# Attention in a transformer block: another order of projections, scores and context, and queries and keys stored token by token

## The chip, the core and the metric

The kernel runs on one core of a Trainium2 chip. The metric is the time of one execution on the device in microseconds (us); less is better. The engines of a core are named as in the profile: PE (TensorE, matrix products; PEld is its weight load), DVE (VectorE), ACT (ScalarE), POOL (GpSimd) and SP (SyncE, which here only issues DMAs). Each engine works through its own queue in order and waits on semaphores for the others.

## The reference

One block of a transformer on 2048 tokens of width 1024, in float32: layer norm, attention, residual, layer norm, gated feed-forward, residual. The attention is unusual: it runs within a token, over the token's 32 heads of width 32, not between tokens. So for every token there is a 32 x 32 matrix of scores, a softmax over it, and a 32 x 32 by 32 x 32 product with the values.

```python
x = L0_attn_hidden_states                       # (1, 2048, 1024)
x = x + attn(_layernorm(x, axis=-1), wq, bq, wk, bk, wv, bv, wl, bl)
x = x + ffn(_layernorm(x, axis=-1), w1, w2, w3)

def attn(hidden_states, ...):
    q = (hidden_states @ wq.T + bq).reshape(B, S, H, D)     # H = D = 32
    k = (hidden_states @ wk.T + bk).reshape(B, S, H, D)
    v = (hidden_states @ wv.T + bv).reshape(B, S, H, D)
    scores = jnp.einsum('bshd,bstd->bsht', q, k) / np.sqrt(D)
    probs = jax.nn.softmax(scores, axis=-1)
    return jnp.einsum('bsht,bstd->bshd', probs, v).reshape(B, S, E)

def ffn(x, w1, w2, w3):                                     # hidden width 2752
    dq1, dq2, dq3 = (nf4_quant_dequant(w) for w in (w1, w2, w3))
    h = silu(x @ dq1.T) * (x @ dq2.T)
    return h @ dq3.T
```

`nf4_quant_dequant` scales each block of 64 weights by its largest magnitude, rounds it to one of 16 values and scales it back.

## The kernel before

The tokens are worked on in 16 tiles of 128 (NT = 16, i is the tile). The program first runs a fast version of the block, in which the three projections use a float32 product with the activations split into a high and a low part (`xh`, `xl`); only if the weights are not what that needs does a second version run. The profile shows the fast one, and the change is in it.

The attention of a tile is made of these steps. The letters are functions in the code, and PE runs their products in exactly the order in which they are called, since PE's order is written by hand; on the other engines a scheduler places the instructions that each step issues, and may move them among each other.

- `prepare(i)`: layer norm of the tile on ACT and POOL, giving `xn`. The tile's input `xt` is loaded three tiles ahead, in `G(i-3,1)`.
- `split(i)`: eight PE transposes of `xn` (L618), which ACT and DVE copy as `xh` (L620) and `xl` (L621).
- `Q(i,n)`, `K(i,n)`, `V(i,n)`: half a projection each (n is the half of the columns), 16 products of 512 columns (L648) into one of four PSUM banks; then `take` on DVE moves the bank to SBUF, transposing blocks of 32 x 32 (L665 for queries and keys, L678 for values), and after the second half adds the bias (L667, L683). There is one buffer each for queries `qd`, keys `kd` and values `vd`.
- `S(i,part)`: scores of half of the tile's tokens, 64 products of 32 x 32 (L696). After the second half follows the softmax: DVE takes the maximum and subtracts it (L733, L735), ACT takes the exponential (L741), DVE transposes (L743), giving `prT`.
- `G(i,part)`: context of half of the tokens, 64 products of 32 x 32 by 32 x 33 (L700; the 33rd column of `vd` is all ones and gives the softmax's sum). After the second half DVE divides by the sum (L758, L760), transposes (L768) and adds the residual (L771); SP stores the result and loads the next input tile; POOL and ACT make the second layer norm (L578 to L585).
- `keep(i)`: eight PE transposes of the normed tile (L511), ACT copies, DVE differences (L527), and stores for the feed-forward.

Scores and context of all tiles share one PSUM tile `at` of four banks: it takes the scores of tile i, then its context, then the scores of tile i+1.

The loop over tiles calls, for i from 3 on:

```python
Q(i, 0); Q(i, 1); flush(1); keep(i - 2); K(i, 0)
G(i - 1, 0); K(i, 1); flush(1); G(i - 1, 1)
V(i, 0); S(i, 0); V(i, 1); flush(1); split(i + 1); S(i, 1); advance(2)
```

Between these steps the weights of the feed-forward are rounded in the background. `advance(n)` issues n x 10/17 turns of that work: a turn is mostly one of eight bands of a weight tile, one pass of ACT (L299) and one of DVE (L305), or a tile's scaling, sixteen small ACT instructions (L259). `flush` issues the four PE transposes of a finished weight tile's half (L219). Every projection, S and G calls `advance(1)`.

After the loop, the first products of the feed-forward (`plain_block`, eight groups of L391, taken one at a time by `next(plain)`) are mixed with the last tile's context and the last two `keep`s. There `held["behind"]` makes the background work wait for the last tile's norm. The feed-forward proper then runs to the end.

Of the kernel before, what the change touches and what calls it, by code (L numbers as in the profile page):

```python
# [16 lines left out]
ALU = mybir.AluOpType  # L17
# [3 lines left out]
P = 128  # L21
S = 2048
E = 1024
NH = 32
D = 32
# [5 lines left out]
NT = S // P  # L31
# [99 lines left out]
def forward(ctx, tc, const, fast, x, wqT, wkT, wvT, qb, kb, vb, w1, w2, w3, out):  # L131
# [113 lines left out]
    def flush(steps=3):  # L245
        for _ in range(steps):
            if pending and next(pending[0], flush) is flush:
                pending.pop(0)
# [108 lines left out]
    def advance(n):  # L357
        lent["turns"] += n * TURN
        while lent["turns"] >= 1:
            lent["turns"] -= 1  # L360
            with turn():
                next(bg, None)
# [80 lines left out]
    def load_op(name, tbp):  # L443
        tag = "T1" if name == "B12" else name
        t = wpool.tile([P, 4, TB], FP, tag=tag, name=f"x{name}")
        nc.sync.dma_start(t, xd[name, tbp])
        ops[tag] = (name, tbp, t)
# [83 lines left out]
    if fast:  # L531
# [78 lines left out]
        def split(i):  # L610

            hi = work.tile([P, KC, P], F32R, tag="xh", name="xh", bufs=2)
            lo = work.tile([P, KC, P], F32R, tag="xl", name="xl", bufs=2)
            src = xn.pop(i)
            for half in range(2):
                pt = bank("pt").rearrange("p (k t) -> p k t", t=P)
                for k in range(4):
                    nc.tensor.transpose(pt[:, k, :], src[:, ts(4 * half + k, P)], ident)  # L618
                ks = ts(half, 4)
                marked(nc.scalar.copy(hi[:, ks], pt))  # L620
                nc.vector.tensor_tensor(lo[:, ks], pt, hi[:, ks].bitcast(FP), ALU.subtract)  # L621
            xs[i] = hi, lo
# [17 lines left out]
                for n in range(2):  # L640
                    take(n, ps[i, n])

        def project(m, i, n, take):

            ps = bank("pj")
            for k in range(KC):
                for part in xs[i]:
                    nc.tensor.matmul(  # L648
                        ps,
                        part[:, k, :],  # L650
                        W[m][k // 2][:, k % 2, ts(n, TB)],
                        start=k == 0 and part is xs[i][0],
                        stop=k == KC - 1 and part is xs[i][1],
                        skip_group_check=True,
                    )
            take(n, ps)
            advance(1)

        def qk(m, i, bias):
            tag = f"{m}d" if i != 1 else "xT1" if m == "q" else "xT0"  # L660
            t = work.tile([P, 32, NH], FP, tag=tag, name=f"{m}d")

            def take(n, ps):
                hs = ts(n, NH // 2)
                nc.vector.transpose(t[:, hs], ps.rearrange("p (h d) -> p h d", d=D))  # L665
                if n:
                    nc.vector.tensor_tensor(  # L667
                        t, t, bias.unsqueeze(2).to_broadcast([P, 32, 32]), ALU.add
                    )

            return t, take
# [21 lines left out]

        def score(at, q, k, part):
            for s, b, n, r in tokens(part):
                nc.tensor.matmul(at[r, b, ts(n, 32)], q[r, :, s], k[r, :, s], start=True, stop=True)  # L696

        def weigh(at, p, part):
            for s, b, n, r in tokens(part):
# [3 lines left out]

        qd, kd, prT, ats = {}, {}, {}, {}

        def Q(i, n):
            if not n:
                qd[i] = qk("q", i, qb_sb)
            project("q", i, n, qd[i][1])

        def K(i, n):
            if not n:
                kd[i] = qk("k", i, kb_sb)
            project("k", i, n, kd[i][1])

        def V(i, n):
            project("v", i, n, take_v)
            if n:
                del xs[i]

        def S(i, part):

            if not part:
                ats[i] = ps_at.tile([P, 4, 512], FP, tag="at", name="sc")
            at = ats[i]
            score(at, qd[i][0], kd[i][0], part)
            advance(1)
            if not part:
                return
            del qd[i], kd[i], ats[i]  # L730
            sc = at[:, :, 0:256].rearrange("p g (s t) -> p g s t", t=NH)
            mx = small.tile([P, 4, 8], FP, tag="mx", name="mx")
            nc.vector.tensor_reduce(mx, sc, AX.X, ALU.max)  # L733
            pr = work.tile([P, 32, NH], FP, tag="pr", name="pr")
            nc.vector.tensor_tensor(  # L735
                pr.rearrange("p (g s) t -> p g s t", g=4),
                sc,
                mx.unsqueeze(3).to_broadcast([P, 4, 8, NH]),
                ALU.subtract,
            )  # L740
            nc.scalar.activation(pr, pr, AF.Exp, scale=1.0 / math.sqrt(D))  # L741
            prT[i] = work.tile([P, 32, NH], FP, tag="prT", name="prT")
            nc.vector.transpose(prT[i], pr)  # L743
# [37 lines left out]
        def keep(i):  # L781
            keep_T(i, x1n.pop(i))
# [36 lines left out]
        G(0, 1)  # L819
        prepare(3)  # L820
        V(1, 0)
        S(1, 0)
        V(1, 1)
        S(1, 1)
        K(2, 1)
        keep(0)
        split(3)
        for i in range(2, NT):
            last = i == NT - 1
            if i > 2:  # L830
                if not last:
                    prepare(i + 1)
                Q(i, 0)
                Q(i, 1)
                flush(1)
                keep(i - 2)
                K(i, 0)
            if last:
                for name in ("B11", "B21"):
                    load_op(name, 0)  # L840
            G(i - 1, 0)
            if i > 2:
                K(i, 1)
            flush(1)
            G(i - 1, 1)
            if last:
                until("2", 0)
                w0 = []
                for n, tag in enumerate(("xh", "xl")):
                    t = work.tile([P, 2, 4, P], FP, tag=tag, name="w0", bufs=2)  # L850
                    nc.sync.dma_start(t, wd["2", 0][:, 2 * n : 2 * n + 2])
                    w0 += [t[:, 0], t[:, 1]]
                for name in ("B12", "B22"):
                    load_op(name, 0)
            V(i, 0)
            S(i, 0)
            V(i, 1)
            flush(1)
            if not last and i > 2:
                split(i + 1)  # L860
            S(i, 1)
            advance(2)
        hook["scale"] = "both"
        left.close()
# [10 lines left out]
        hook["pool"] = (ps_tail, "pj", 2)  # L875

        plain = plain_block(w0, 0)
        next(plain)
        advance(1)
        next(plain)  # L880
        keep(NT - 2)
        advance(1)
        next(plain)
        G(NT - 1, 0)
        next(plain)
        G(NT - 1, 1)
        held["behind"] = hook["normed"]
        for _ in range(3):
            next(plain)
            advance(2)  # L890
        keep(NT - 1)
        hs = {0: next(plain)}
        advance(2)
        sweep.close()
        sweep_at.close()
        right.close()
# [806 lines left out]
```

## Time and profile before

| | |
|---|---|
| time, three runs | 2238.79, 2229.97, 2224.99 us (median 2229.97) |
| time of the profiled execution | 2238.77 us |
| its span, first to last instruction | 2236.9 us |
| PE busy | 2167.1 us (97%) |
| DVE busy | 1378.0 us (62%) |
| ACT busy | 1287.2 us (58%) |
| POOL busy | 302.2 us (14%) |
| mean granted clock of PE | 0.984 |

How to read it: busy is the time in which the engine had at least one instruction under way. The profile's line numbers are those of the kernel. In a group, `out<-in` names the tiles written and read; "x4096 | 67.6, 225 | 21.3 <-..." stands for 4096 records, 67.6 us busy in all, 225 ns for one, and 21.3 us in which the engine was idle just before them, with what ended that idleness. A product in float32 leaves two records, so half a tile's 64 small products are 128 records. PE's clock is granted in two steps here, full and half, and is listed as a share.

### The profile page before, as it was taken

The page shows a single profiled execution, that of the slowest core. Times are in us where ns is not written, and L with a number is a line of the kernel's source. Part 1 is how long each engine was busy: PE and PEld are TensorE (multiplying, and loading weights), DVE is VectorE, ACT ScalarE, POOL GpSimd, SP SyncE. Part 2 cuts the span into 40 slices and gives each one's busy share as a digit, 9 for nine tenths or more (in the row PEclk, how much of TensorE's full clock was granted, in tenths as well). Part 3 has the DMA queues.
Part 4 walks back from the last instruction along what each step waited for, and adds up shares of the span by engine and source line. Part 5 has one row for each costly group of instructions (what it writes and reads, how often), then busy time and mean ns, then how long its engine had stood idle before and what let it go on. Part 6 is the DMA issues. An engine that isn't in the chain of part 4 may idle for free.

```text
span 2236.9 us, 35174 instructions
## 1 busy us (share of the span) xinstructions
PE 2167.1 (97%) x14193; PEld 1173.4 (52%) x14193; DVE 1378.0 (62%) x1600; ACT 1287.2 (58%) x2529; POOL 302.2 (14%) x425
## 2 busy tenths in 40 slices
PE   7999999989989999999999999999999999999998
PEld 6777787778534444444444444444444444444432
DVE  6778777786377565576565665756666656653022
ACT  7566665662285756758657666676586575511200
POOL 2010010100001203104012021040130210401300
PEclk9899999999999999999999999999999999999999
DMA  8132323234558837579349596394883776974972
GB/s 292 40 101 93 117 65 115 95 98 144 216 193 294 172 141 180 163 280 252 137 141 210 206 283 149 124 214 162 308 207 133 181 190 224 269 236 136 255 290 96
DMA packets 154683, 402.72 MB, mean 180 GB/s; under 512 B 13648, under 2 KB 67920, under 8 KB 137360
## 3 DMA queue, kind: packets, MB, share of 16 engines
q1 hardware_dynamic: 113808, 326.92, 40.7%
q0 software_dynamic: 40704, 73.47, 19.7%
q8 instruction: 113, 1.85, 0.3%
q14 instruction: 58, 0.48, 0.1%
HBM read 227.07 MB, written 173.28 MB: 179 GB/s over the span
## 4 chain that ended last, share of the span: by engine, by line
PE 48%; issue 14%; DMA 5%; DVE 2%; ACT 2%; POOL 1%; DVEq 0%; POOLq 0%; ACTq 0%; SPq 0%
PE z L391 18%; PE q L391 8%; PE z L1511 8%; PE rr L391 4%; PE y L1511 4%; DMA wd<-wop 3%; DMA x1d<-acc 3%; PE r L1511 2%; PE po L1594 1%; PE ptw L219 1%; DVE r L305 1%; PE po L1605 1%; ACT wn L259 1%; POOL x1d L1526 1%; ACT acc L1524 0%
## 5 line engine op out<-in xcount | busy, mean ns | idle before, releaser
L299 ACT ACTIVATE sg<-wn 128x1024 int8<-128x1024 f32 (+1 forms) x520 | 542.5, 1052 | 138.6 <-DVE r L305 128.0
L305 DVE CUSTOM_DVE_ANT_0 r<-r,sg 128x1024 f32<-128x1024 f32 (+1 forms) x455 | 551.4, 1212 | 31.1 <-ACT sg L299 12.0
L1526 POOL DMA_DIRECT2D x1d<-acc x280 | 244.8, 900 | 1253.2 <-ACT acc L1524 1220.0
L391 PE MATMUL z<-xB,w 128*128 128x512 f32 x720 | 320.9, 595 | 3.5 <-ACT u L1430 2.1
L391 PE MATMUL z<-xT,w 128*128 128x512 f32 x656 | 297.5, 596 | 8.3 <-ACT g L1416 8.2
L391 PE MATMUL q<-xT,w 128*128 128x512 f32 x656 | 291.1, 592 | 0.0
L1511 PE MATMUL z<-w,h 128*128 128x512 f32 x496 | 230.5, 593 | 1.7 <-ACT acc L1524 1.5
L391 PEld LDWEIGHTS z<-xB,w 128*128 128x128 f32 x720 | 135.0, 191 | 163.5 <-issue 157.1
L259 ACT ACTIVATE wn<-wn,rc 128x64 f32<-128x64 f32 x736 | 189.0, 340 | 40.2 <-DVE rc L279 40.1
L391 PEld LDWEIGHTS z<-xT,w 128*128 128x128 f32 x656 | 124.1, 192 | 159.7 <-issue 149.0
L391 PEld LDWEIGHTS q<-xT,w 128*128 128x128 f32 x656 | 123.1, 190 | 148.4 <-issue 146.3
L303 DVE TENSOR_SCALAR r<-sg 128x1024 f32<-128x1024 int8 (+1 forms) x65 | 44.5, 684 | 194.7 <-PE ptw L219 194.4
L1511 PEld LDWEIGHTS z<-w,h 128*128 128x128 f32 x496 | 92.6, 190 | 112.7 <-issue 102.8
L1511 PE MATMUL y<-w,h 128*128 128x512 f32 x320 | 148.8, 592 | 0.0
L391 PE MATMUL rr<-xB,w 128*128 128x512 f32 x328 | 147.5, 592 | 0.0
L220 ACT COPY wop<-ptw 128x512 f32<-128x512 f32 (+1 forms) x130 | 76.2, 586 | 113.2 <-PE ptw L219 87.7
L1524 ACT COPY acc<-z 128x512 f32<-128x512 f32 x160 | 92.6, 581 | 70.7 <-PE z L1511 54.5
L1426 DVE TENSOR_TENSOR g<-g,rr 128x512 f32<-128x512 f32 x41 | 27.9, 681 | 168.4 <-PE rr L391 168.3
L259 ACT ACTIVATE r<-r,am 128x64 f32<-128x64 f32 x440 | 113.0, 343 | 8.9 <-DVE r L305 8.6
L271 DVE TENSOR_REDUCE am<-wn 128x16 f32<-128x1024 f32 (+1 forms) x65 | 78.6, 1209 | 48.0 <-ACT r L259 45.6
L648 PE MATMUL pj<-wv,xh 128*128 128x512 f32 x240 | 105.1, 438 | 1.2 <-issue 1.2
L648 PE MATMUL pj<-wv,xl 128*128 128x512 f32 x240 | 101.0, 421 | 0.0
(144 smaller groups left out, 2730.3 us busy)
## 6 DMA issues: line engine op xcount, KB each, us to landing
x1d<-acc POOLq DMA_DIRECT2D x280, 256.0 KB, 6.8
wd<-wop SPq DMA_DIRECT2D x31, 2048.0 KB, 8.5
w<-wd SPq DMA_DIRECT2D x41, 1280.0 KB, 7.0
wn<-in_w_dram SPq DMA_DIRECT2D x63, 512.0 KB, 6.0
xT<-xdT SPq DMA_DIRECT2D x28, 1024.0 KB, 7.6
xB<-xdB SPq DMA_DIRECT2D x24, 1024.0 KB, 6.7
w<-wd SPq DMA_DIRECT2D x44, 512.0 KB, 4.3
w<-wd SPq DMA_DIRECT2D x10, 1536.0 KB, 8.3
```

The source lines that it names most:

```text
L220: nc.scalar.copy(o[:q, first + half], pt[:q])
L259: nc.scalar.mul(dst[:, ts(n, BLOCK)], src[:, ts(n, BLOCK)], by[:, n : n + 1])
L271: nc.vector.tensor_reduce(am[:, :nb], v.rearrange("p (b e) -> p b e", e=BLOCK), AX.X, ALU.max, apply_absolute_value=True,)
L299: nc.scalar.activation(t, v, AF.Copy, bias=bias, scale=scale)
L303: nc.vector.tensor_scalar(r, t, top, low, ALU.min, ALU.max)
L305: nc.vector._custom_dve(TENSOR_ADD_SAT, out=r, in0=r, in1=t, s0=top, s1=low)
L391: nc.tensor.matmul(dst, w[:, k, :], xop[:, k, :], start=start and k == 0, stop=stop and k == 3, skip_group_check=True,)
L648: nc.tensor.matmul(ps, part[:, k, :], W[m][k // 2][:, k % 2, ts(n, TB)], start=k == 0 and part is xs[i][0], stop=k == KC - 1 and part is x ...
L1426: nc.vector.tensor_tensor(self.g0, self.g0, r, ALU.add)
L1511: nc.tensor.matmul(dst, side[n][:, ts(q, P)], w3T[g[2 * m]][:, W3[n]], start=start and m == 0, stop=stop and m == 1, skip_group_check=True,)
L1524: nc.scalar.copy(t, src)
L1526: nc.gpsimd.dma_start(x1d[8 * tbp + 2 * q + j][n], t, accum_op=ALU.add)
```

## The change

Two things change in the fast version.

First, queries and keys are stored with the heads side by side for each token. Before, `t[:, head, token]` holds the 32 words of one token 32 words apart; after, `t[:, token, head]` holds them next to each other. The transposes on DVE, which still read the bank in order, now write with a step of 32 words; the bias is broadcast along the other axis; the score products read consecutive words.

Second, the order. In the loop the second half of the scores of tile i-1 moves into `Q(i,0)`, between its products and its `take` (the argument `first`); both halves of K come ahead of G; `split(i+1)` moves between the halves of G; both halves of V come ahead of `S(i,0)`. The opening (tiles 1 and 2) and the end follow: the last scores fall among the first products of the feed-forward, `piece(n)` calls `advance(n)` after each of these, two `flush`es are added, and `held["behind"]` is no longer set. The line numbers of the changed kernel are two higher from L665 on (L667 for L665, L698 for L696, L702 for L700).

```diff
-        def project(m, i, n, take):
+        def project(m, i, n, take, first=lambda: None):
...
+            first()
             take(n, ps)
             advance(1)
...
             t = work.tile([P, 32, NH], FP, tag=tag, name=f"{m}d")
+            by_head = t.rearrange("p s h -> p h s")
...
-                nc.vector.transpose(t[:, hs], ps.rearrange("p (h d) -> p h d", d=D))
+                nc.vector.transpose(by_head[:, hs], ps.rearrange("p (h d) -> p h d", d=D))
                 if n:
                     nc.vector.tensor_tensor(
-                        t, t, bias.unsqueeze(2).to_broadcast([P, 32, 32]), ALU.add
+                        t, t, bias.unsqueeze(1).to_broadcast([P, 32, 32]), ALU.add
                     )
...
-                nc.tensor.matmul(at[r, b, ts(n, 32)], q[r, :, s], k[r, :, s], start=True, stop=True)
+                nc.tensor.matmul(at[r, b, ts(n, 32)], q[r, s, :], k[r, s, :], start=True, stop=True)
...
         V(1, 0)
+        V(1, 1)
         S(1, 0)
-        V(1, 1)
+        split(3)
         S(1, 1)
         K(2, 1)
+        G(1, 0)
         keep(0)
-        split(3)
+        G(1, 1)
         for i in range(2, NT):
             last = i == NT - 1
             if i > 2:
                 if not last:
                     prepare(i + 1)
-                Q(i, 0)
+                Q(i, 0, lambda: S(i - 1, 1))
                 Q(i, 1)
                 flush(1)
                 keep(i - 2)
                 K(i, 0)
-            if last:
-                for name in ("B11", "B21"):
-                    load_op(name, 0)
-            G(i - 1, 0)
-            if i > 2:
                 K(i, 1)
-            flush(1)
-            G(i - 1, 1)
+                flush(1)
+                if last:
+                    for name in ("B11", "B21"):
+                        load_op(name, 0)
+                G(i - 1, 0)
+                if not last:
+                    split(i + 1)
+                G(i - 1, 1)
+            V(i, 0)
...
-            V(i, 0)
-            S(i, 0)
             V(i, 1)
             flush(1)
-            if not last and i > 2:
-                split(i + 1)
-            S(i, 1)
+            S(i, 0)
             advance(2)
...
         plain = plain_block(w0, 0)
-        next(plain)
-        advance(1)
-        next(plain)
+
+        def piece(n):
+            got = next(plain)
+            advance(n)
+            return got
+
+        piece(1)
+        S(NT - 1, 1)
+        piece(2)
         keep(NT - 2)
-        advance(1)
-        next(plain)
+        piece(2)
+        piece(2)
         G(NT - 1, 0)
-        next(plain)
+        piece(2)
+        flush(1)
         G(NT - 1, 1)
-        held["behind"] = hook["normed"]
-        for _ in range(3):
-            next(plain)
-            advance(2)
+        piece(1)
+        flush(1)
+        piece(1)
+        hs = {0: piece(1)}
         keep(NT - 1)
-        hs = {0: next(plain)}
-        advance(2)
```

More of the change, by code (lines that the diff above doesn't have):

```diff
@@ L704, in forward, with Q @@
         qd, kd, prT, ats = {}, {}, {}, {}
-        def Q(i, n):
+        def Q(i, n, first=lambda: None):
             if not n:
                 qd[i] = qk("q", i, qb_sb)
-            project("q", i, n, qd[i][1])
+            project("q", i, n, qd[i][1], first)
         def K(i, n):
```

## The prediction

> **What bounds the kernel now.** I began with the page, cut the span into stages where TensorE (PE) changes its work, and then read PE's own timeline, its groups, and the groups of VectorE (DVE) inside the attention loop.
>
> ```profile
> span 2236.9 us, 35174 instructions
> ...
> PE 2167.1 (97%) x14193; PEld 1173.4 (52%) x14193; DVE 1378.0 (62%) x1600; ACT 1287.2 (58%) x2529; POOL 302.2 (14%) x425
> ```
>
> PE is busy 97% of the span, so the question is where the other 70 us lie, and which PE time is slower than it need be. The columns of the next view: stretch and its length, busy time (instructions) of PE, weight loads, DVE, ACT, POOL, then the granted clock, DMA share and GB/s.
>
> ```profile
> 0.00:120.23 120.23, 104.75 (x1633) 84.61 (x1633) 82.28 (x100) 79.06 (x163) 15.77 (x42) 0.91 0.47 164
> 120.23:543.91 423.68, 399.39 (x7565) 325.84 (x7560) 334.64 (x374) 253.04 (x515) 39.24 (x96) 0.97 0.30 98
> 543.91:580.38 36.47, 32.95 (x628) 26.65 (x621) 21.38 (x24) 5.21 (x7) 1.18 (x4) 0.95 0.83 290
> 580.38:629.95 49.57, 41.33 (x362) 20.09 (x356) 25.39 (x29) 24.02 (x44) 1.18 (x4) 0.91 0.51 169
> 629.95:2204.90 1574.95, 1564.18 (x3963) 708.54 (x3964) 904.09 (x1060) 925.85 (x1801) 244.82 (x280) 1.00 0.70 202
> ```
>
> From 629.95 us on, in the feed-forward part, PE is busy 99.3% at full clock, and the change does not touch it: these 1607 us to the end of the span stay. All that can move lies before. The second row is twelve turns of the attention loop (tiles 3 to 14), 35.3 us each, with 24.3 us of PE idleness and 0.97 of the clock.
>
> ```profile
> L696 PE MATMUL sc<-kd,qd 32*32 32x32 f32 x4096 | 67.6, 225 | 21.3 <-DVE pw L760 10.7 <-issue 8.4 <-DVE rc L278 2.2
> ...
> L696 PEld LDWEIGHTS sc<-kd,qd 32*32 32x32 f32 x4096 | 63.1, 145 | 31.2 <-issue 27.8 <-PE pj L648 3.4
> ...
> L700 PE MATMUL cx<-vd,prT 32*32 32x33 f32 x4096 | 43.9, 196 | 0.7 <-issue 0.7
> ...
> L700 PEld LDWEIGHTS cx<-vd,prT 32*32 32x32 f32 x4096 | 39.9, 106 | 12.3 <-issue 11.0 <-DVE qd L665 0.7 <-DVE qd L667 0.4
> ```
>
> Score products (L696) and context products (L700) are 4096 records each, with the same tile positions in the same order. The scores read both operands one word in 32, the context reads consecutive words. The scores take 67.6 us, the context 43.9 us although it has one column more. The scores also hold 21.3 us of idleness.
>
> ```profile
> 314.75 1.29 PE L700 MATMUL cx<-vd,prT 32*32 32x33 f32 x128
> ...
> 319.89 2.03 PE L696 MATMUL sc<-kd,qd 32*32 32x32 f32 x128
> ```
>
> This is one half tile of each at full clock: 1.29 and 2.03 us. And the wait:
>
> ```profile
> 217.49 2.05 PE L696 MATMUL sc<-kd,qd 32*32 32x32 f32 x128 [2.98 <-DVE pw L760]
> ```
>
> The scores of tile i wait until DVE has read the context of tile i-1 out of the one PSUM tile "at"; only V(i,0), 3.75 us, lies between.
>
> **Part 1: score products on consecutive words.** 32 half tiles x (2.03 - 1.29) = 24 us off PE, 1.5 us of each loop turn. The bounds are 0 (the layout is not what makes L696 slow) and 24; nothing else differs between the two groups, so I take 24.
>
> **Part 2: the price, DVE's transposes.** Four transposes a tile (L665) now write one word in 32. No row of before has contiguous reading with strided writing. The rows around it:
>
> ```profile
> L678 DVE STREAM_TRANSPOSE vd<-pj 128x512 f32<-128x512 f32 x24 | 27.2, 1131 | 22.7 <-PE pj L648 22.7
> L768 DVE STREAM_TRANSPOSE cx<-pw 128x1024 f32<-128x1024 f32 x12 | 26.9, 2242 | 0.1
> L665 DVE STREAM_TRANSPOSE kd<-pj 128x512 f32<-128x512 f32 x24 | 17.1, 711 | 16.8 <-PE pj L648 16.8
> ...
> L743 DVE STREAM_TRANSPOSE prT<-pr 128x1024 f32<-128x1024 f32 x12 | 14.9, 1245 | 15.2 <-ACT pr L741 15.2
> ```
>
> With both sides contiguous (L665, L743) it is 711 ns for 512 words and 1245 for 1024; with both strided (L678, L768) 1131 and 2242. So each of the four costs between 0 and 0.42 us more, 0 to 1.7 us a turn. I take the upper end: the strided rows double, whichever side does it. The bias add stays at 1.22 us, since L683 adds a bias broadcast the new way in 1.22 us. This is off PE's path only while DVE has room. DVE is busy 334.6/12 = 27.9 us a turn and, in order, waits 3.0 us a turn for others than PE (in the loop: prT for the exponential 15.2, xU for its DMA 10.1, am 4.9, xl 3.5, sum 33.7 of 424, and some 2 more for wop). So DVE needs 30.9 us a turn before and up to 32.6 after.
>
> [...]
>
> **Part 3: the order.** Before, a turn is Q Q keep K G K G V S V split S; after, Q S' Q keep K K G split G V V S, where S' is the second half of the scores of tile i-1. What each move does:
> - S(i,0) now has V(i,0), V(i,1) and a weight transpose between it and G(i-1,1): 7.5 us and more instead of 3.75. The longest wait for pw was 2.98 us, so the 10.7 us go; with DVE 1.7 us later there is still a margin of about 1 us.
> - split(i+1) now stands 11 us ahead of Q(i+1,0); the waits for xh (3.3 us) and xl (1.5 us) go.
> - The softmax chain from S' to G(i-1,0) keeps its cover: three projections and keep, 12.2 us, as before.
> - keep(i-2) has less: from the end of G(i-2,1) to keep, PE had 21.4 us of work and now has 18.1. The chain there (DVE up to L771, POOL, two passes of ACT) took 10.5 us for the context that ended at 316.0 and 16.3 us for the one at 383.9. It fits, but barely.
> - 5.8 us of "issue" waits inside the small products stay.
> - The half-rate clock: seven stretches in the loop, 27.4 us at 0.50, cost 13.5 us. Five follow a wait of 1 to 3 us beside a score block, which mostly goes. But G, split, G with a flush ahead is now 4.0 us without a wide product. Before, 4.26 us of such work up to 156.73 was followed by 0.50 from 156.9 to 160.3, and 4.2 us up to 228.5 was not. One such stretch costs 1.7 us; I count two in the loop, bounds 0 and 12 (20 us).
>
> [...]
>
> **Sum of the loop.** PE's need per turn: (423.7 - 24.3 - 13.5)/12 = 32.2 us before, less 1.5 is 30.7 after. DVE's need is 30.9 to 32.6. The turn will lie near the larger with its upper transposes: 32.4 us, where heavy and light turns of the background work (DVE 23.9 to 31.4 us busy) partly even out. Gain 12 x (35.3 - 32.4) = 35 us.
>
> **Around the loop.** *Opening:* split(3) now stands ahead of S(1,1) and K(2,1). Its input xn is ready at 99.4 us (before: PE waited 2.98 us and then ran at 0.50 from 98.8 to 109.1). PE arrives at about 88, waits 10 us, and has S(1,1), K(2,1), keep still to do: 2 us lost. *Last tile (36.5 us):* a score half moves on and no split is left; 29.5 us of PE work and 2 of issue waits, 5 us won. *Change to feed-forward (49.57 us):*
>
> ```profile
> 618.11 3.60 PE L391 MATMUL q<-xT,w 128*128 128x512 f32 x8
> 629.95 6.05 PE L391 MATMUL z<-xT,w 128*128 128x512 f32 x8 [8.25 <-ACT g L1416]
> ```
>
> The copy of g stood behind a burst of background work on ACT, which was held until the last norm. The change drops that hold and spreads the work; in the built order, however, ACT now has two bands and ten scalings between the two passes of the last norm, and they wait for DVE's last three bands. keep(15) then starts some 6 us late, and the copy of g follows sixteen scalings. PE's work is 40.6 us; with the wait 47.5. I count 2 us won. On SP's queue the loads for the feed-forward keep their places behind the stores of tile 13.
>
> Sum: 35 - 2 + 5 + 2 = 40 us off the profiled execution's 2238.8 (2236.9 span and 1.9 around it): 2199. The median of the runs shown is 2230.0, 8.8 lower than the profiled one. A part of that difference may be the very waits and half-rate stretches that the change removes, so I take half of it: 2195.
>
> **Rivals.**
> 1. *DVE does not notice* (transposes cost nothing): DVE 30.9, PE 30.7, a turn of 31.3; gain 48 - 2 + 5 + 2 = 53, that is about 2180. For it: L665 reads contiguously. Against: nothing shows which side the price of L678 comes from.
> 2. *DVE becomes the bound*: the heavy turns (31.4 busy + 1.7 + 3 = 36) do not even out, or the clock falls each turn. A turn of 34 us gives 12 x 1.3 = 16, and in all about 18 to 20 us: 2214, within 1%.
> 3. *Slower*: the chain from G(i-2,1) to keep decides. From 18.1 us on, each further us is one us of PE wait in every turn. The turn is then the chain plus keep, two K, flush, G, split, G, 12.6 us; it equals 35.3 at a chain of 22.7, which is 6.4 us over the longest measured. At 25.5 the loop loses 12 x 2.8 = 34 us, the rest gives 5 back: about 2260. For it: ACT and DVE are in order and background bands stand between pw, cx and the norm. Against: 16.3 us is the most that the rows I read had, and DVE's extra is 1.7.
> 4. *The layout is not the reason for L696's 2.03 us*: then 24 us are missing, and 2214 is reached from the order alone.
>
> **How the numbers follow.** Forecast 0.50, rival 1 0.18, rivals 2 and 4 together 0.23, rival 3 0.09. The range reaches from rival 1 without the opening's 2 us and the 5.8 us of issue waits (2172) to a loop without gain, 2230. About 1% (22 us) can be told apart: faster by more takes the forecast, rival 1 and little else, 0.69; within 1% 0.22; slower 0.09.
>
> **What would show it.** Right: L698 at 1.29 us a half tile, no wait for pw, L667 near 1.13 us, turns of 32 to 33 us, Q(3,0) at about 122 us. Wrong: score blocks still at 2.0; waits of keep's transposes (L511) for the norm, or a granted clock below 0.97 in the loop with no idleness ahead of it; a long wait for L1423 at the change to feed-forward.

## The result and the profile after: 2266 us, slower by 1.5%

| | before | after |
|---|---|---|
| median of six runs each, on the same chip | 2235.11 us | 2265.94 us (2263.31 to 2274.16) |
| ratio, 95% interval | | 1.0151, 1.0124 to 1.0177 |
| profiled execution | 2238.77 us | 2268.73 us |

The forecast was 2195 us with a range up to 2230: wrong in sign and out of its range. The page of the changed kernel begins:

```profile
span 2266.9 us, 35201 instructions
...
PE 2153.2 (95%) x14193; PEld 1157.2 (51%) x14193; DVE 1389.3 (61%) x1599; ACT 1287.7 (57%) x2545; POOL 319.7 (14%) x425
```

PE is busy 13.9 us less (the faster scores, less what a lower clock takes back) and the span is 30.0 us longer. PE waits 44 us more. Cut at the same products as the kernel before (first product of Q(3,0), of Q(15,0), the first feed-forward product among the last scores, the product that waited for g), the columns as in the prediction's table of stretches:

```profile
0.00:127.71 127.71, 100.06 (x1500) 79.99 (x1500) 84.68 (x99) 76.33 (x159) 15.14 (x41) 0.88 0.43 153
127.71:563.18 435.47, 387.83 (x7572) 312.31 (x7564) 341.79 (x371) 260.08 (x537) 52.80 (x92) 0.95 0.29 94
563.18:603.80 40.62, 33.09 (x628) 26.73 (x621) 31.27 (x35) 15.75 (x31) 4.01 (x8) 0.87 0.72 245
603.80:656.23 52.43, 43.51 (x492) 22.13 (x485) 23.77 (x27) 25.32 (x54) 2.96 (x4) 0.93 0.50 170
```

The opening is 7.5 us longer (127.71 for 120.23), the loop 11.8 (435.47 for 423.68), the last tile 4.1 (40.62 for 36.47), the change to the feed-forward 2.9 (52.43 for 49.57), and the rest to the end of the span 3.7 (2266.9 - 656.23 for 2236.9 - 629.95). So every stage lost. In the loop PE was busy 11.6 us less and waited 23.3 us more.

The groups of the loop (busy, ns of one, then the idle time before):

```profile
L702 PE MATMUL cx<-vd,prT 32*32 32x33 f32 x3072 | 35.3, 198 | 21.4 <-issue 21.0 <-DVE prT L745 0.4
...
L698 PE MATMUL sc<-kd,qd 32*32 32x32 f32 x3080 | 31.1, 193 | 0.0
...
L667 DVE STREAM_TRANSPOSE qd<-pj 128x512 f32<-128x512 f32 x24 | 26.2, 1091 | 2.4 <-PE pj L648 2.4
L667 DVE STREAM_TRANSPOSE kd<-pj 128x512 f32<-128x512 f32 x24 | 25.9, 1078 | 7.7 <-PE pj L648 7.7
```

The scores (L698) now cost what the context costs and wait for nothing; the transposes that write with a stride cost 1.09 us instead of 0.71. Both are as the prediction had them. The idle time has moved. PE's waits in the loop, as engine, tile and line that waited, what released it, us in total, times, longest; first the kernel before:

```profile
PE sc L696 <- DVE pw L760: 10.7, 7, 3.0
PE sc L696 <- issue: 4.6, 4, 1.9
PE pj L648 <- ACT xh L620: 3.3, 6, 0.8
PE sc L696 <- DVE rc L278: 2.2, 1, 2.2
PE pj L648 <- DVE xl L621: 1.5, 6, 0.3
PE pj L648 <- issue: 1.2, 1, 1.2
PE pj L648 <- ACT wop L220: 0.6, 1, 0.6
```

And the changed kernel:

```profile
PE cx L702 <- issue: 21.0, 10, 5.5
PE pj L648 <- ACT wop L220: 10.1, 4, 4.4
PE pj L648 <- DVE qd L667: 10.0, 5, 4.3
PE pt L511 <- ACT cx L585: 3.6, 3, 2.3
PE pt L618 <- DVE rc L278: 2.4, 1, 2.4
PE cx L702 <- DVE prT L745: 0.4, 1, 0.4
```

The waits for pw (10.7 us), xh and xl (4.8 us) are gone. In their place stand "issue" waits inside the context products, and waits of K's first product for a PSUM bank, which comes free when DVE has taken Q out (qd) or ACT has copied weight transposes (wop).

**What the issue waits are.** One of them, in PE's timeline (start, length, instruction, idle time before):

```profile
371.80 0.97 PE L702 MATMUL cx<-vd,prT 32*32 32x33 f32 x90
378.29 0.77 PE L702 MATMUL cx<-vd,prT 32*32 32x33 f32 x38 [5.51 <-issue]
```

A half tile stops after 90 of its 128 records, and no input ends the wait. The page lists instruction fetches as queues of their own; this one fits PE's instructions (packets, MB, share):

```profile
q8 instruction: 113, 1.85, 0.3%
```

113 packets of 16 KB for 14193 products and 14193 weight loads is one packet for 251 instructions. I counted PE's instructions (products, weight loads and the semaphore instructions between them) in order of time, in the traces of all 20 kernels of this study. All 202 issue waits over 0.8 us begin at instruction 193 or 194 of a group of 256 (in the changed kernel the fourteen stand a whole multiple of 256 instructions apart, give or take one), and each ended 2.2 to 3.2 us after a 16 KB packet of this queue had started. Apart from the last two packets of each trace, none started while PE had more than 301 instructions left before the group that the packet brings, so fetching runs about one group ahead. A half tile of S or G is 64 products of 32 x 32, which is 256 instructions in 1.3 us; a wide half projection is 32 in 3.75 us. So G, split, G uses up more than two groups within 3.6 us. PE runs dry in the second G, in 10 of 12 turns: for 0.8 to 1.6 us where the packet had started before PE stopped, and for 3.2 to 5.5 us in the three turns where it started after. Why those three started late is not shown.

### The profile page after: what moved, and what is told of

The parts are those of the page before. It is cut to its first block, busy times and chain, and to the rows that moved or that the text cites. A ratio compares the mean times of both kernels' runs of the same rounds, so it can differ in the third digit from the quotient of the medians.

```text
span 2266.9 us, 35201 instructions
## 1 busy us (share of the span) xinstructions
PE 2153.2 (95%) x14193; PEld 1157.2 (51%) x14193; DVE 1389.3 (61%) x1599; ACT 1287.7 (57%) x2545; POOL 319.7 (14%) x425
## 3 DMA queue, kind: packets, MB, share of 16 engines
q0 software_dynamic: 40704, 73.47, 19.2%
## 4 chain that ended last, share of the span: by engine, by line
PE 37%; issue 36%; DVE 9%; ACT 7%; DMA 7%; POOL 4%; SPq 0%; POOLq 0%; DVEq 0%; ACTq 0%
PE z L391 10%; PE pj L648 6%; DMA x1d<-acc 5%; PE z L1518 5%; PE q L391 4%; PE y L1518 3%; DVE r L305 2%; PE rr L391 2%; POOL x1d L1533 2%; PE po L1601 1%; PE r L1518 1%; ACT wn L259 1%; ACT r L259 1%; DVE cx L770 1%; PE pj L631 1%
## 5 line engine op out<-in xcount | busy, mean ns | idle before, releaser
L648 PE MATMUL pj<-wk,xh 128*128 128x512 f32 x224 | 96.9, 433 | 22.7 <-DVE qd L667 12.5
```

Source lines behind the costliest of these rows:

```text
L648: nc.tensor.matmul(ps, part[:, k, :], W[m][k // 2][:, k % 2, ts(n, TB)], start=k == 0 and part is xs[i][0], stop=k == KC - 1 and part is x ...
```

## The experiments

Eighteen kernels were run, three rounds each, against the kernel before on the same chip. "Ends" are the opening (all ahead of the loop) and the tail (all behind it).

| run | scores, transposes | order | median us | ratio (95%) |
|---|---|---|---|---|
| e1 | new, new | before | 2247.07 | 1.0058 (1.0037-1.0079) |
| e5 | new, old | before | 2236.51 | 1.0005 (0.9992-1.0017) |
| e6 | old, new | before | 2251.12 | 1.0069 (1.0045-1.0094) |
| e7 | old, old | before, split early | 2224.80 | 0.9947 (0.9928-0.9966) |
| e4 | new, new | before, split early | 2230.65 | 0.9989 (0.9977-1.0001) |
| e15 | old, old | split early, S(i,0) later | 2233.07 | 0.9998 (0.9987-1.0009) |
| e2 | old, old | all changed | 2264.01 | 1.0142 (1.0114-1.0170) |
| e8 | old, old | loop changed, ends before | 2236.85 | 1.0009 (0.9995-1.0024) |
| e9 | old, old | e8, K between the G | 2233.00 | 0.9995 (0.9977-1.0013) |
| e18 | old, old | e8, V between the G | 2232.42 | 0.9980 (0.9969-0.9991) |
| e11 | new, new | loop changed, ends before | 2238.10 | 1.0015 (1.0001-1.0030) |
| e10 | new, new | e11, K between the G | 2241.15 | 1.0022 (1.0000-1.0044) |
| e3 | new, new | all changed, K between the G | 2262.03 | 1.0124 (1.0098-1.0150) |
| e12 | new, new | all changed, lost flush back | 2255.05 | 1.0078 (1.0053-1.0104) |
| e13 | new, new | opening before | 2246.48 | 1.0043 (1.0026-1.0060) |
| e14 | new, new | flush back, tail before | 2243.05 | 1.0036 (1.0018-1.0053) |
| e16 | new, new | e13 with held["behind"] | 2248.13 | 1.0065 (1.0044-1.0087) |
| e17 | new, new | e13 with the tail's old pace | 2235.79 | 0.9997 (0.9984-1.0010) |

Most single executions of a kernel lie within 5 us of their median, a few up to 11, so a profile's stages are read for their waits, and the sizes come from the medians. The score products of e5 and e6 pair other words than the attention does; the number and size of the instructions are the same.

### Layout or order (e1 to e4)

Theory A: the order is at fault. Theory B: the layout is.

e1 is the kernel before with the three layout edits of the change (`by_head`, `unsqueeze(1)`, `q[r, s, :]`) and no others.

> The order of before, with queries and keys stored token by token. Theory A (the order is at fault: three small blocks in a row, G split G, use up TensorE's instruction pages of 256, and the way from G to keep and K has less cover): score halves at 1.29 us, transposes at 1.08 us, no issue wait inside G, few waits of K for DVE; 24 us off the scores, some given back to DVE: 2210 to 2222 us, faster than before by 0.6 to 1.1%. Theory B (the layout is at fault: four transposes of 0.38 us more a tile make DVE late, and K waits for its PSUM bank): waits of K for DVE or ACT as in the changed kernel, some 20 us in the loop, and a time at or above before, 2235 to 2250.

2247.07 us: theory B's place, but not by theory B's waits. No wait for qd or kd stands in its loop; what grew is Q's wait for xh, 14.5 us for 3.3 before. The layout alone costs 12 us, though it takes 24 us off PE.

e2 is the changed kernel without those three edits.

> The order of the changed kernel, with queries and keys stored by head as before. Theory A: the issue waits in the second half of G stay (15 to 25 us in the loop) and the scores cost 24 us more than in the changed kernel: 2275 to 2290 us. Theory B: DVE has its 1.5 us a turn back, the waits of K go, and the time falls to 2235 to 2250.

2264.01 us, between the two ranges and nearer to A's. The order alone costs nearly all (29 us), and the layout on top of it nothing more. The issue waits of its loop are 21.0 us, as with the layout.

e3 is the changed kernel with a wide block between the two halves of G:

```diff
                 K(i, 0)
+                G(i - 1, 0)
                 K(i, 1)
                 flush(1)
...
-                G(i - 1, 0)
                 if not last:
                     split(i + 1)
                 G(i - 1, 1)
```

> The changed kernel with K(i,1) moved between the halves of G (K G K split G), all else as it is. Theory A, instruction pages: the issue waits of 21.0 us in the loop fall below 8; what is won is partly lost to G's wait for the softmax, whose cover falls from 12.2 to 8.5 us (1 to 2 us a turn): 2245 to 2262 us against 2266. Theory B: issue waits are chance, the time stays at 2260 to 2272 or rises by the softmax wait alone.

The issue waits in G fell from 21.0 to 3.8 us and the loop from 435.5 to 424.9 us in the profile. So the waits follow theory A. The time does not decide: the whole gained 4 us only, and 2262.03 lies at the upper edge of A's range and within B's. The waits for prT and qd in its loop came to 13.6 and 13.2 us, and all behind the loop took 5.9 us more in this profile than in the changed kernel's.

e4 is e1 with the split moved ahead of the first scores:

```diff
             V(i, 0)
+            if not last and i > 2:
+                split(i + 1)
             S(i, 0)
             V(i, 1)
             flush(1)
-            if not last and i > 2:
-                split(i + 1)
             S(i, 1)
```

> The order of before with one step moved (split(i+1) from ahead of S(i,1) to ahead of S(i,0)), and the token by token layout. It takes the waits of Q for xh and xl (4.8 us in the loop) and gives the reading of at by DVE 1 us more cover (part of 10.7 us), with every small block still apart from the next by a wide product or a split. Theory A: 2200 to 2215 us, the fastest of all. Theory B: as the layout alone, 2235 to 2250.

2230.65 us: 16 us better than e1, and still not faster than before. Neither theory by itself was enough, so I took each apart.

### Taking the layout apart (e5, e6, e7)

e5 changes one line, the operands of the score products, to `q[r, s, :], k[r, s, :]`; e6 is e1 with that line as before.

> The kernel before, its transposes and its order untouched; only the score products read 32 consecutive words of the tile that is there (so they pair other words than the reference does: what is computed is not the attention, the instructions are the same in number and size). Theory 1 (the layout costs because the transposes of L667 take 1.09 instead of 0.71 us): nothing is slower here and the 24 us of the scores come in nearly whole, 2208 to 2218 us. Theory 2 (the layout costs because the faster score products only bring PE sooner to waits for the pieces of split and for the take of a bank, which ACT and DVE end): little is gained, 2222 to 2236 us, with more than 10 us of waits for ACT xh in the loop, as in the run of the layout alone (14.5).

> The kernel before with the token layout, but score products that read it with the old stride (again other words than the reference pairs; same number and size of instructions). The transposes of queries and keys are the slow ones, the scores too. Theory 1: the whole cost of the layout without its gain, 2255 to 2275 us. Theory 2: the slow scores cover the slow transposes, 2233 to 2245 us.

Faster scores by themselves gain nothing: 1.0005, where theory 1 wanted 17 to 27 us. The first of PE's waits in the loop of e5:

```profile
PE pj L648 <- ACT xh L620: 17.1, 9, 3.5
PE sc L696 <- issue: 5.9, 4, 2.6
PE sc L696 <- DVE pw L760: 5.7, 5, 2.3
```

S(i,1) stands between split(i+1) and Q(i+1,0). Its 2.03 us were the cover under which ACT copied xh. At 1.29 us Q comes sooner, and waits (17.1 us, 3.3 before).

e6 fell between the theories, 2251.12: the slower transposes cost 16 us, with the slow scores still there as cover. Their 18 us of DVE time in the loop (48 x 0.38) were priced at nothing. In the profiles the loop is 8.3 us longer than before (432.0 for 423.7), 3.6 us of it waits and 4.8 us PE's busy time at a lower clock (0.95 for 0.97), and the opening is 2.9 us longer; the rest of the 16 us these two profiles don't show (that of before is 3.7 us over its median). By the ratios this and e5 add up to e1 within 4 us.

e7 is e4's edit on the old layout.

> The kernel before, old layout, with split(i+1) moved ahead of S(i,0) and nothing else. Taking the split out of its place behind V(i,1) gave 16 us together with the token layout (2247 to 2231). If that came from waits that the old layout has too (xh and xl 4.8 us, pw 10.7 us in the loop), this one gains 5 to 12 us, 2222 to 2229 us. If the early split only repaired what the slow transposes had broken, it gains nothing: 2230 to 2238 us.

2224.80 us, ratio 0.9947: of the versions that compute the attention, the only one here that is clearly faster than both kernels. The waits for xh and xl are gone, those for pw fall from 10.7 to 6.8 us. So e4's 16 us were not all a repair of the layout: 10 are to be had without it, and with this order too the layout costs 6 us (e4 less e7).

### The loop without the ends (e8 to e11, e18)

e8 has the changed loop, the opening of the kernel before and its tail, with S(15,1) right behind the loop; e11 is the same with the layout.

> Old layout; the changed order in the loop alone, with the opening and the tail as before (S(15,1) directly behind the loop). If the order costs in the loop (issue waits of 21 us in G and waits for a PSUM bank of 10 us, less the waits that go): about 2240 us (2236 to 2246), so 6 of the 30 us of the order's run. If all of it costs through what the loop leaves for opening and tail: 2230 to 2236 us, with the rest of the 30 us in those two.

> The changed kernel with the opening and the tail of the kernel before (changed loop, token layout). The loop's order by itself was 2237. If opening and tail of the change cost the most of its 30 us: 2236 to 2248 us. If it is the loop, where the layout and the order together lose more than each: 2254 to 2268 us.

2236.85 and 2238.10 us. e8 lies 0.9 us inside the range in which the loop's order costs, but its ratio (1.0009, 0.9995 to 1.0024) shows no cost. So the changed loop is as fast as the old one, with either layout, and **28 of the 31 us come from the changed ends** (one of their parts takes effect inside the loop, see e12). That is the reverse of what I held after e2. PE's waits in the loop of e11:

```profile
PE cx L702 <- issue: 19.4, 10, 5.6
PE pj L648 <- DVE qd L667: 9.6, 5, 5.0
PE pj L648 <- ACT wop L220: 3.1, 2, 1.9
PE pj L648 <- ACT xT L512: 2.4, 1, 2.4
PE pt L618 <- DVE rc L278: 2.4, 1, 2.4
PE pt L511 <- ACT cx L585: 1.7, 2, 1.4
PE pj L648 <- issue: 0.4, 1, 0.4
```

A ledger of the twelve turns shows where the expected gain went. The half-rate cost is half of PE's busy time at 0.50; PE's work is its busy time less that.

| loop, us | before | e11 | after |
|---|---|---|---|
| PE's work at full clock | 386.4 | 369.9 | 370.3 |
| half-rate clock | 13.0 | 10.4 | 17.6 |
| waits for pw, xh, xl | 15.5 | 0 | 0 |
| issue waits | 5.8 | 19.8 | 21.0 |
| projections' waits for qd, kd, wop, xT | 0.6 | 15.4 | 20.1 |
| other waits | 2.4 | 4.4 | 6.5 |
| sum | 423.7 | 419.9 | 435.5 |

Of the 34.6 us that go in e11 (16.5 of work, 2.6 of half-rate clock and 15.5 of waits), 30.8 come back as other waits.

e9 and e18 ask whether the issue waits can be had back: e9 moves K(i,1), as e3 did, and e18 moves V(i,0) between the halves.

> The run of the changed loop alone (old layout, opening and tail as before), with K(i,1) moved between the two halves of G. If the changed order costs because three small blocks in a row (G, split, G, and in the last tile S, S) use up PE's instructions faster than they are fetched: the issue waits (18.3 us in the loop, 8.8 in the last tile) fall below 5 and 2 us and the time is 2216 to 2226 us. If instead the waits for prT and for the take of Q (13.6 and 13.2 us in the run of the whole change with K between) come in their place, because G(i-1,1) and so K(i+1) come later: 2230 to 2240 us.

> The changed loop alone (old layout, old ends; 2237 us) with V(i,0) moved between the halves of G, so that G, V, split, G has a wide block in it. The issue waits (18.3 us) should fall below 5 us, as they did with K there. If that is a gain that stays: 2219 to 2227 us. If the cover is only moved, because S(i,0) then has one wide block less behind G(i-1,1) and waits for pw again (10.7 us before), and K for its bank: 2228 to 2238 us.

In e18, V(i,0) overwrites half of the values that G(i-1,1) still has to read, so those products take other values. The longest of PE's waits in the loop of e8:

```profile
PE cx L701 <- issue: 18.3, 10, 4.9
PE pj L648 <- DVE qd L666: 2.9, 1, 2.9
```

In the loop of e9:

```profile
PE cx L701 <- DVE prT L744: 17.0, 6, 8.7
...
PE cx L701 <- issue: 2.8, 2, 2.4
```

In the loop of e18:

```profile
PE cx L701 <- DVE vd L679: 21.9, 12, 3.2
PE cx L701 <- issue: 0.4, 1, 0.4
```

A wide block between the halves takes the issue waits in G away each time (18.3 to 2.8 and to 0.4; e9 has 3.0 more ahead of a projection), which shows that they come from small blocks in a row. And each time another wait of the same size stands there: with K, the first G comes one block sooner than the softmax; with V, the second G waits until DVE has taken V into the only vd. The rivals named for both runs held in kind: e9 gained 4 us, e18 4 us. The one price they did not name was vd, not pw.

e10 is e9 with the layout.

> The same with the token layout. If the layout costs only where it brings PE sooner to a split that is not ready (17.1 us of waits for xh in the run of the faster scores alone), this order, whose split is two wide blocks ahead of its use, gets a good part of the 24 us: 2200 to 2214 us. If DVE and ACT are what PE waits for here (the transposes cost 16 us by themselves in the order before), it is 2220 to 2240 us, with waits for qd and prT of over 15 us in the loop.

2241.15 us, 8 more than e9 and 1 over the range of "DVE and ACT are what PE waits for"; prT is waited for 19.8 us, qd 10.4. In five orders the layout cost 12 us (e1 against before), 6 (e4, e7), 1 (e11, e8), 8 (e10, e9) and 2 (the changed kernel, e2); the 1 and the 2 are not clear of the noise. It never gained.

### The ends (e12 to e14, e16, e17)

In the opening, PE's timeline of the changed kernel shows what split(3) ahead of S(1,1) does:

```profile
91.95 1.29 PE L698 MATMUL sc<-kd,qd 32*32 32x32 f32 x128
102.35 1.97 PE L618 MATMUL pt<-ident,xn 128*128 128x128 f32 x8 [9.10 <-ACT xn L585]
104.25 1.93 PE L698 MATMUL sc<-kd,qd 32*32 32x32 f32 x128
```

The norm of tile 3 ends between 99.4 and 104.7 us in all 20 traces, whatever PE's order (102.3 here, 99.4 before). Before, PE had the scores, K(2,1) and keep(0) to do until then; now it waits 9.1 us, and does them later, partly at half rate. Then G(1,0), moved ahead of keep(0), waits 2.28 us for prT.

The diff has a smaller change there: tile 1's halves of G had a `flush(1)` between them, which is now inside `if i > 2`. e12 puts it back:

```diff
         G(1, 0)
         keep(0)
+        flush(1)
         G(1, 1)
```

> The changed kernel with the one flush(1) back that its opening lost (tile 1's, between the halves of G), so that the pieces of background work stand in the loop where they stand before. If the loop of the change is 11 us dearer than the same loop behind the old opening (430 against 419 us, old layout) because the background work stands half a piece later: 2252 to 2260 us. If the opening's order itself does it: 2262 to 2270 us.

2255.05 us (four executions): one call of flush is worth 11 us by the medians and 16 by the ratios, and it removes no work, it only does it sooner. In the profiles it lies in the loop, which takes 418.2 us here and 419.2 in e14, which has the flush too, instead of 435.5, with the same steps called in the same order. (Behind the loop e12's profile is 7.4 us longer than the changed kernel's.)

With the flush lost, each half piece of the background's transposes comes one flush later, but not for long: PE's order of blocks differs in the first three turns of the loop only and is the same from the fourth on. The price lies in the second and third turn. As a stretch of these two turns and PE's waits in it, first the changed kernel, then e12:

```profile
159.74:245.97 86.23, 70.36 (x1272) 56.88 (x1264) 61.80 (x70) 44.09 (x95) 9.92 (x17) 0.86 0.27 87
PE cx L702 <- issue: 8.0, 2, 4.8
PE pj L648 <- ACT wop L220: 4.4, 1, 4.4
PE pj L648 <- DVE qd L667: 3.5, 1, 3.5
```

```profile
163.92:232.75 68.83, 63.52 (x1269) 51.19 (x1261) 62.30 (x68) 50.13 (x109) 9.71 (x16) 0.98 0.32 106
PE pj L648 <- ACT xT L512: 2.4, 1, 2.4
PE cx L702 <- issue: 1.7, 2, 0.8
PE pj L648 <- DVE qd L667: 1.3, 2, 0.8
```

The difference, 17.4 us, is all that the loop gains (17.3): 10.6 us of waits and 6.8 us of PE's busy time at a lower clock (0.86 for 0.98). The other ten turns together come out even. e2, which lost the flush too, has 41.9 and 39.8 us in the same two turns, e8 with it 33.3 and 33.2. Why that place is the worse one, beyond these waits, was not taken further.

e13 puts back the opening alone, e14 the tail and the flush.

> The changed kernel with only its opening put back; changed loop, token layout, changed tail. With both ends put back it was 2238 us, with both as changed 2266, with the lost flush alone put back 2255. If the changed tail costs something by itself (the stages behind the loop are 7 to 14 us longer in the runs that have it), this is 2244 to 2253 us. If the opening made all of the 28 us, it is 2236 to 2242 us.

> The changed kernel with the flush(1) of tile 1 put back and the tail of the kernel before; the opening's order (split(3) ahead of S(1,1), G(1,0) ahead of keep(0)) stays changed. If that order costs its wait for xn (9.1 instead of 3.0 us), for prT (2.3 us) and a longer half-rate stretch: 2243 to 2250 us, some 8 us above the run with both ends put back. If the tail was free and the order of the opening costs the rest: 2252 to 2258 us.

2246.48 and 2243.05 us, both inside the ranges in which tail and opening's order cost: against e11 the tail costs 8 us and the opening's order 5. With the flush (11) and e11's own 3 that is 27 of the 31 us; with the flush by its ratios 32.

For the tail, e16 sets `held["behind"] = hook["normed"]` again behind G(15,1), on top of e13. e17 leaves that out and takes away two flushes and the two units of `advance` that the tail has more than before:

```diff
         S(NT - 1, 1)
-        piece(2)
+        piece(1)
         keep(NT - 2)
-        piece(2)
+        piece(1)
         piece(2)
         G(NT - 1, 0)
         piece(2)
-        flush(1)
         G(NT - 1, 1)
         piece(1)
-        flush(1)
         piece(1)
```

> The run with the old opening, changed loop and changed tail (2246), with the line back that the change took out of the tail: held["behind"], which keeps the background's scalings on ACT behind the norm of the last tile. If the tail costs its 8 us because those scalings get in ahead of that norm (keep(15) waits 6.5 us for cx): the wait shrinks and the time is 2238 to 2243 us. If not: 2244 to 2249 us.

> The same run (2246) with the two flushes and the two extra units of advance taken out of the tail, so that as much background work is done when the feed-forward begins as before; the order of the tail's blocks stays changed. If the tail costs because the background work behind it stands elsewhere (waits for a weight at about 2020 us, 4.0, for u 3.4, for wop 2.5): those go and the time is 2237 to 2242 us. If the order of the blocks does it: 2244 to 2249 us.

e16 gained nothing (2248.13), although keep(15)'s wait for cx, 6.54 us in e13, is gone: a wait of 6.61 us for g stands in its place. e17 is 2235.79, 1 us below its range: the pace of the background work was the tail's whole cost. Where in the feed-forward it lies is not shown: e13 and the changed kernel wait 4.0 and 3.8 us for a weight's load at about 2020 us, which e17's profile doesn't, but that profile is its slowest execution (2243.21), and its wait for u, which should have gone too, is 5.8 us (3.4 in e13). Flushes and units of advance were not told apart.

### Another arrangement (e15)

e15 is e7 with S(i,0) behind V(i,1):

```diff
             V(i, 0)
             if not last and i > 2:
                 split(i + 1)
-            S(i, 0)
             V(i, 1)
+            S(i, 0)
             flush(1)
             S(i, 1)
```

> Old layout, the order before with two moves: split(i+1) ahead of V(i,1), and S(i,0) behind V(i,1), so that S(i,0) has two wide blocks behind G(i-1,1) to cover the division of pw. The early split alone gave 2225 us, with 6.8 us of waits for pw left in the loop. If that wait goes and the two score blocks, which take 4.1 us together in the old layout, don't run out of instructions: 2215 to 2222 us. If two score blocks in a row wait for instructions like the two G of the change: 2224 to 2236 us.

2233.07 us, in the rival's range. The waits for pw are gone from its loop (6.8 in e7), and ten short issue waits (8.2 us) stand in the two score blocks in a row. Its profile is its fastest execution of ten (2225.84), so its stages don't show the 8 us by which it is slower than e7; that stays open.

## Why the prediction was wrong, point by point

By the medians, the loop with its layout was to gain 35 us and cost 3 (e11); the ends were to gain 5 and cost 28, of which the lost flush is 11, the tail's pace 8 and the opening's order 5. So both parts failed, at the terms named below.

Against the profiled execution the steps gave -40 us and the trace shows +30.0. The 70 us of difference are 47 in the loop, 5.5 in the opening, 9 in the last tile, 5 at the change to the feed-forward and 3.7 behind it.

- **Part 1** was right in size (1.29 us a half tile), wrong in worth. e5 has it alone and gains nothing.
- **Part 2** was right in size (0.38 us of the 0.42 taken). "Off PE's path only while DVE has room" was the condition, and DVE's mean need of 32.6 us in a turn of 35 seemed to meet it. e6 shows 16 us for it. As I read it, the transposes stand right behind a projection, and the next take, copy and exponential wait for their turn in order: room in the mean is not room at that place. That path itself was not tested apart.
- **Part 3, waits that go:** right. pw, xh and xl are at zero.
- **Part 3, covers:** the softmax chain kept its cover (0.4 us for prT). keep waited 3.6 us in all, so "it fits, but barely" held.
- **Part 3, "5.8 us of issue waits stay"** is the step that failed by the most in the loop's order: 21.0 us. I counted G, split, G as 4.0 us without a wide product and asked only what the clock makes of it. What it does is use up PE's instructions. The prediction's own rows had the sign of it: 8.4 us of issue waits ahead of score products.
- **Part 3, clock:** 27.4 us at half rate were to shrink to two stretches, 6.9 us; there were 41.0. In PE's busy time that is a cost of 17.6 us where 3.4 were counted. Each of the eight stretches begins during a wait of 1.8 to 5.5 us or within 0.6 us of its end, and the waits had not gone but moved.
- **Sum of the loop:** "the turn will lie near the larger" of PE's and DVE's needs. This is the rule that failed as a whole. PE's work is 30.9 us a turn in the changed kernel (370.3/12), near the 30.7 worked out, and the turn 36.3. Nothing in this study got the mean turn below 34.3 us (e15's loop, 412.1 in its fastest execution). As I read the waits, they are the places where a chain through DVE and ACT meets PE's fixed order, and a wait that is removed lets PE run into the next one.
- **Opening:** -2 was priced by hand for split(3), with PE arriving at 88 us and waiting 10. The wait was 9.10, for 2.98 before, which is 6.1 of the 7.5 us lost (2.9 of them because the norm itself ended later in this execution): the step saw the wait and then did not take the difference. The lost flush was not counted at all, though it stands in the diff; e12 gives it 11 us.
- **Last tile** (+5, measured -4.1): an issue wait of 4.85 us in G(14,1) and a wait of 2.49 for qd, for the 2 us that were allowed, and 10.2 us at half rate beside them, which were not counted.
- **Change to the feed-forward** (+2, measured -2.9). keep(15) was to start "some 6 us late":

```profile
646.23 1.97 PE L511 MATMUL pt<-ident,cx 128*128 128x128 f32 x8 [6.58 <-ACT cx L585]
```

It did. The half-rate clock that followed (643.9 to 650.8) was not counted, nor an issue wait of 2.34 us in S(15,1).
- **"These 1607 us stay":** they grew by 3.7 us here. e13 and e17 differ by 10.7 us in all, by the background's pace alone.

Of the rivals, the third had nearly the right time (2260) by the wrong way: keep's chain never decided. (Its longest in the loop before was 19.2 us, behind the context that ended at 488.97, and not the 16.3 of the rows read.) The second, DVE as the bound, comes nearest for the layout, and ended too low because it kept the gains of the order. Two sums of the rivals are a little off, and nothing rests on them: the terms of the second give 21 us, not 18 to 20, and the 24 us that the fourth leaves out lead to 2219, not 2214.

## What to carry to other kernels

When an engine with a fixed order waits in many places, time taken off it is not yet time won: for each wait removed, ask what the engine meets next and how late that is, and try the part alone (here 24 us of faster products were worth nothing, and moving one split 10 us). Count every background step that an edit drops or adds at the ends, since the steps behind it shift: one flush was 11 us, in two turns of the loop. Look at "issue" waits in the trace before putting blocks of small instructions side by side, and compare instructions per microsecond with what the instruction queue brings (here the small blocks took 256 in 1.3 us, and PE went on 2.2 to 3.2 us after a packet had started).

## What was not expected of the hardware

- PE runs out of instructions: 202 waits over 0.8 us in 20 traces, all at instruction 193 or 194 of 256. Two context blocks around a split, each at about 200 instructions per us (256 in 1.3 us), had it in 10 of the 12 turns of the changed loop. The waits were 0.8 to 6.7 us long.
- A DVE transpose of 128 x 512 float32 words took 1.08 to 1.09 us where it writes with a step of 32 words and reads in order (L667 of the changed kernel), 0.71 us where both are in order (L665 before).
- The granted clock fell after short waits. In the changed kernel a wait of 2.36 us in a split (443.6 to 445.9, "DVE rc", with 2.6 us of small products ahead of it) was followed by a granted clock of 0.50 from 446.0 to 449.4.
